# Three moves in the issue order of a two-layer attention and expert kernel: the first context's load, the experts' ranks, the last attention output

## The chip, the cores and the metric

The kernel runs on one core of a Trainium2 chip. The core has five engines that work side by side and wait for each other by semaphores: PE (TensorE, matrix products and transposes into PSUM), DVE (VectorE), ACT (ScalarE), POOL (GpSimd) and SP (SyncE, which here only issues transfers). PEld in a profile is PE's loading of weights, which overlaps its matmuls. The metric is device time in microseconds for one execution, as the median of the runs.

## The reference

The inputs are 32 sequences of 64 rows of 512 numbers (2048 rows in all), and a context of the same shape. Two layers follow each other, each a cross-attention and a feed-forward part, each added to the rows:

```
x = x + attention0(layernorm(x), context)     # 32 heads of 128, 8 key/value groups
x = x + ffn0(layernorm(x))                    # up 1024, relu squared, down, a latent branch, layernorm
x = x + attention1(rmsnorm(layernorm(x)), context)   # 32 heads of 16, 8 key/value groups
x = x + experts(layernorm(x))                 # 8 experts, each row takes its best two
```

The expert part, which most of the change touches, is

```python
logits = x @ W_gate + b_gate
_, top_idx = jax.lax.top_k(logits, TOP_K)        # TOP_K = 2
y_all = jax.nn.relu(jnp.einsum('bsd,edh->bseh', x, W_e) + b_e)
y = jnp.take_along_axis(y_all, top_idx[..., None], axis=2)
return y.mean(axis=2)
```

## The kernel before

The 2048 rows are four chunks of 512 (`c`), each chunk four tiles of 128 rows (`xs[i]`), which stay in SBUF from the first load to the end. All numbers are float32.

**Start.** SP issues the loads in their written order (L187 to 193): the four x tiles of chunk 0, the first group's weights by `load_attn0` (keys `wk`, queries `wq`, values `wv`, output `wo`), then the context of chunk 0 (`load_ctx`, 1 MB, the transposed context in four blocks of 128 by 512), then chunk 1's rows and context, then the rest. PE begins with the transposes of chunk 0's normalized rows (`attn0_in`, pt_a), goes on to keys (`attn0_keys`, pk_a) and values (`attn0_values`, pv_a), which multiply the context, then to seven quarters of a query product in Strassen's form (`attn0_queries`, pqx_a, pqy_a, pqz_a, pqv_a), whose sums of weight quarters POOL makes (`left_sums` for `wq`, `right_sums` for `wo`). DVE closes the query quarters into qT_a (L500), copies the values (L478), and makes the row statistics of later chunks (`row_stats`).

**The second attention and the routing.** A loop over 33 batches (`i`, from L1317 on; `c, b = divmod(i, 8)`) is a pipeline written out by hand. In iteration i come, in this order: the masked keys for batch i+2 (POOL), the scores of batch i (PE sixteen small matmuls sc_b; DVE maximum and subtraction, mx_b and at_b; ACT the exponential), the transposes of batch i-1 (pt_v), one half of a query product for the next chunk (`attn1_queries`, pq_b), the routing step of chunk c-1 that a table names for this b, the row work of chunk c+2, the mixing of batch i-1 (`attn1_mix`: PE po, ACT a copy, logarithm and exponential, POOL four instructions L994 to L998), the output product of an earlier pair of batches (`attn1_out`: PE pp, DVE the addition into x, L1012), and up to two scatters from a list of waiting ones (`route_row`). In the last chunk (c = 3) there are no queries left, and `attn1_out` comes every second iteration as a whole.

The routing of a chunk has these steps (`route_step`): normalize rows (`rows0`, `rows2`), transpose them (`turn0`, `turn2`), multiply by the gate (`logits`, gp_e), then `ranks` and `places`. `ranks` is `route_keep`: four transposes (lg_e) and eight dependent DVE instructions from the logits to keep_e, which marks the two best experts of each row. `places` is `route_places`: two small matmuls (cnt_e) that count the rows ahead of each row in its expert's list, the running sums on DVE, and at_e, the row numbers for the scatters. Each scatter (`route_row`, xg<-...,at_e) is an indirect transfer that POOL issues. Chunks 0 to 2 form the first group of lists, chunk 3 the second.

**The expert blocks.** After the loop `load_rows` reads the sorted rows back (xr<-xg, on SP, after all scatters of the group), `block_turn` transposes a block of 128 rows (px, ACT copies it to xT), and `block_expert` multiplies it by its expert's weights (py). At m = 0 the output product of the last tile (`attn1_out(NC * TT - 1, ...)`) is issued behind the first block's transposes. 46 blocks follow each other; their results are gathered and added.

**What sets the order.** A scheduler orders each engine's instructions at compile time by its own estimate of times, lower positions in the program first. `pin` (and `accumulate_next`) keeps an instruction behind the one written before it on its engine. The matmuls, the routing on DVE, and the mixing on POOL are pinned; the statistics, the additions of L1012, and the loads on SP are not. PSUM tiles are handed out in turn: "tr" (transposes, logits, counts) has two buffers, "mm" (products) two in this part.

## Time and profile before

| what | us |
|---|---|
| median of 3 runs | 2020.13 (2019.36 to 2022.64) |
| the profiled execution | 2020.86 |
| its span, first to last instruction | 2019.2 |
| PE busy | 1939.5 (96%) |
| DVE busy | 1011.8 (50%) |
| ACT busy | 494.5 (24%) |
| POOL busy | 474.4 (23%) |
| DMA from HBM / to HBM | 94.44 MB / 58.20 MB |

Starts in a timeline are counted from the first instruction. A group's line gives its start, its length, engine, line of the code, operation and tiles, how many instructions were merged, and in brackets how long the engine had been idle and which instruction ended that. The chain of work that ended last is 91% PE and 5% DVE. The page in 40 slices shows where the engines have gaps (each digit is a tenth of a slice of 50.5 us):

```
PE   6999999999999999999999999999999999869995
DVE  8445445445456445345345355365546676652324
POOL 5010010010032110110111120144136545541024
```

The first attention runs to about 1241 us (its last output product), the first feed-forward part to about 1513, the batches of the second attention from 1560 to about 1808, the expert blocks to 1996, and the last gathers and additions to 2019.

### The profile page before, as it was taken

Reading aid. Unit: us, or ns where it says so; the run is one execution under the profiler, and the core shown is the slowest. Engines: PE = TensorE matmul, PEld = TensorE weight load, DVE = VectorE, ACT = ScalarE, POOL = GpSimd, SP = SyncE. Lnnn points to the kernel's source line nnn. Section 1 sums busy time; section 2 is a strip of 40 time slices with the busy share of each in tenths; the row PEclk is TensorE's granted clock in tenths of the full one; section 3 lists DMA queues with packets and bytes.
Section 4 is the critical chain, followed back from the end, with each engine's and each line's share of the span. In section 5 each row is a group of like instructions: output and inputs, shape, how many; then the busy total and the mean of one; then the engine's idle time right before and its main releaser. Section 6 shows DMA issues by size and latency. Waiting matters only on the chain.

```text
span 2019.2 us, 26458 instructions
## 1 busy us (share of the span) xinstructions
PE 1939.5 (96%) x10576; PEld 1537.1 (76%) x10576; DVE 1011.8 (50%) x1961; ACT 494.5 (24%) x935; POOL 474.4 (23%) x502
## 2 busy tenths in 40 slices
PE   6999999999999999999999999999999999869995
PEld 5888888888888888888888887778787767545442
DVE  8445445445456445345345355365546676652324
ACT  1211211211212211111111112221113656433221
POOL 5010010010032110110111120144136545541024
PEclk9999999999999999999999999999999999889998
DMA  9993110110120110110110013000014002225457
GB/s 319 284 294 106 35 53 18 35 53 20 54 74 8 45 37 17 52 39 15 52 42 13 21 58 105 1 11 1 1 46 163 17 22 69 84 84 177 155 165 233
DMA packets 138233, 155.39 MB, mean 77 GB/s; under 512 B 5120, under 2 KB 88896, under 8 KB 138112
## 3 DMA queue, kind: packets, MB, share of 16 engines
q1 hardware_dynamic: 126096, 124.53, 19.8%
q0 software_dynamic: 5392, 17.11, 2.6%
q10 hardware_dynamic: 6624, 12.06, 1.6%
q8 instruction: 85, 1.39, 0.3%
q14 instruction: 36, 0.29, 0.0%
HBM read 94.44 MB, written 58.20 MB: 76 GB/s over the span
## 4 chain that ended last, share of the span: by engine, by line
PE 91%; DVE 5%; ACT 1%; DMA 1%; POOL 1%; issue 1%; POOLq 0%; SPq 0%; DVEq 0%; ACTq 0%
PE ppx_o L424 11%; PE pqx_a L424 8%; PE py L105 8%; PE sc_a L105 6%; PE pv_a L105 5%; PE ppz_o L424 5%; PE pqz_a L424 5%; PE pk_a L105 5%; PE po_o L105 3%; PE pp L105 3%; PE pdx_f L424 3%; PE ppy_o L424 3%; PE pqy_a L424 3%; PE pqv_a L424 3%; PE phx_f L424 2%; PE pq_b L105 2%
## 5 line engine op out<-in xcount | busy, mean ns | idle before, releaser
L105 PE MATMUL py<-arena,xT 128*128 x368 | 165.7, 593 | 0.0
L406 POOL TENSOR_TENSOR arena<-weights 128x512 f32<-128x512 f32 x16 | 20.7, 1295 | 563.2 <-PE ppz_o L424 563.2
L365 ACT ACTIVATE at_a<-at_a 128x512 f32<-128x512 f32 x64 | 40.4, 631 | 444.0 <-DVE at_a L364 444.0
L105 PEld LDWEIGHTS pv_a<-weights,arena 128*128 128x128 f32 x1024 | 119.4, 192 | 15.3 <-issue 15.3
L424 PE MATMUL ppx_o<-weights,oT_o 128*128 128x256 f32 x512 | 122.8, 383 | 0.1
L424 PE MATMUL pqz_a<-arena 128*128 128x256 f32 x512 | 121.0, 379 | 1.8 <-DVE qT_a L500 1.8
L105 PE MATMUL pk_a<-arena,weights 128*128 128x512 f32 x256 | 117.7, 603 | 3.6 <-issue 3.6
L424 PE MATMUL pqx_a<-arena,weights 128*128 128x256 f32 x512 | 121.0, 379 | 0.0
L105 PEld LDWEIGHTS sc_a<-kT_a,qT_a 128*128 128x128 f32 x1024 | 119.4, 192 | 1.7
L493 ACT ACTIVATE u_a<-pqx_a,bq 128x256 f32<-128x256 f32 x192 | 80.5, 470 | 163.2 <-PE pqx_a L424 163.2
L105 PE MATMUL pv_a<-weights,arena 128*128 128x128 f32 x1024 | 119.5, 275 | 0.0
L105 PE MATMUL sc_a<-kT_a,qT_a 128*128 128x64 f32 x1024 | 117.9, 273 | 0.0
L105 PEld LDWEIGHTS py<-arena,xT 128*128 128x128 f32 x368 | 66.3, 190 | 65.5 <-issue 65.5
L478 DVE COPY v_a<-pv_a 128x512 f32<-128x512 f32 x32 | 22.1, 690 | 179.8 <-PE pv_a L105 179.8
L584 DVE TENSOR_TENSOR x<-ppx_o,x 128x512 f32<-128x512 f32 x128 | 86.8, 678 | 45.7 <-PE ppx_o L424 43.9
L424 PEld LDWEIGHTS pqz_a<-arena 128*128 128x128 f32 x512 | 97.2, 190 | 15.3 <-issue 2.2
L424 PEld LDWEIGHTS ppx_o<-weights,oT_o 128*128 128x128 f32 x512 | 94.8, 190 | 12.0 <-ACT oT_o L574 0.5
L424 PEld LDWEIGHTS pqx_a<-arena,weights 128*128 128x128 f32 x512 | 94.8, 190 | 11.6
L500 DVE TENSOR_TENSOR qT_a<-pqz_a,u_a 128x512 f32<-128x512 f32 x64 | 44.2, 691 | 112.3 <-ACT u_a L493 80.3
L1217 DVE TENSOR_TENSOR y<-py,weights 128x512 f32<-128x512 f32 x46 | 31.8, 691 | 119.7 <-PE py L105 119.3
L105 PEld LDWEIGHTS pk_a<-arena,weights 128*128 128x128 f32 x256 | 49.3, 194 | 52.9 <-issue 51.5
L396 POOL TENSOR_TENSOR arena<-weights 128x512 f32<-128x512 f32 x18 | 23.2, 1290 | 243.5 <-PE pqz_a L424 240.5
(337 smaller groups left out, 3823.2 us busy)
## 6 DMA issues: line engine op xcount, KB each, us to landing
xg<-zero SPq DMA_DIRECT2D x8, 3072.0 KB, 18.0
weights<-in_Wq SPq DMA_DIRECT2D x16, 1024.0 KB, 5.3
weights<-in_Wo SPq DMA_DIRECT2D x16, 1024.0 KB, 5.2
xr<-xg SPq DMA_DIRECT2D x46, 256.0 KB, 3.4
yg<-y ACTq DMA_DIRECT2D x46, 256.0 KB, 3.0
weights<-in_Wkv SPq DMA_DIRECT2D x32, 256.0 KB, 2.8
arena<-in_ctxT SPq DMA_DIRECT2D x8, 1024.0 KB, 5.1
xg<-zero SPq DMA_DIRECT2D x8, 1024.0 KB, 13.0
```

What stands on the lines that cost most here:

```text
L105: nc.tensor.matmul(ps, lhsT, rhs, start=(i == 0), stop=(i == len(pairs) - 1))
L365: nc.scalar.activation(dst, dst, AF.Exp, scale=scale)
L396: engine.tensor_tensor(s1, a21, a22, ALU.add)
L406: engine.tensor_tensor(t1, b12, b11, ALU.subtract)
L424: nc.tensor.matmul(ps[:, m, :], left[:, k, m * P : (m + 1) * P], right[:, k, :], start=first and m == i == k == 0, stop=i == len(pairs) - ...
L478: nc.vector.tensor_copy(v, pv)
L493: nc.scalar.activation(u[:, m * 256 : (m + 1) * 256], ps[:, m * 256 : (m + 1) * 256], AF.Identity, bias=bq[:, 4 * g + 2 * heads + m : 4 * ...
L500: nc.vector.tensor_tensor(q5[:, heads, :, 4 * half : 4 * half + 4, :], ps.rearrange("p (m b q) -> p m b q", m=2, q=64), u.rearrange("p (m ...
L584: nc.vector.tensor_tensor(dst, ps.rearrange("p (m n) -> p m n", m=2), dst, ALU.add)
L1217: pin(nc.vector.tensor_tensor(y, py, be1[:, bass.ds(v[1], 1), :], ALU.add))
```

## The change

Three edits, with no change to what is computed.

1. `load_attn0` gets a hook behind the key weights, and loads `wv` ahead of `wq` in every visit. For the first visit the hook loads chunk 0's context. The order at the start was x0 to x3, wk, wq, wv, wo, ctx0, x4...; it becomes x0 to x3, wk, ctx0, wv, wq, wo, x4....
2. `ranks` leaves the two routing tables. It is issued one batch earlier, at the end of the iteration with b = 5 (b = 3 for the last chunk of queries), behind `attn1_out`, while `places` stays in the iteration with b = 6 (b = 4). Three chunks pass through this; chunk 3's routing runs between the expert blocks and is as before.
3. At m = 0 `attn1_out` of the last tile is issued ahead of `block_turn`, no longer behind it.

```diff
-    def load_attn0(g, slot):
+    def load_attn0(g, slot, between=lambda: None):
         ...
         nc.sync.dma_start(wk, rows(a["Wkv"][:, g * P : (g + 1) * P]))
+        between()
+        nc.sync.dma_start(wv, rows(a["Wkv"][:, (NG + g) * P : (NG + g + 1) * P]))
         nc.sync.dma_start(wq, rows(a["Wq"][:, g * 512 : (g + 1) * 512]))
-        nc.sync.dma_start(wv, rows(a["Wkv"][:, (NG + g) * P : (NG + g + 1) * P]))
         nc.sync.dma_start(wo, rows(a["Wo"][g * 512 : (g + 1) * 512, :]))
         ...
         if c == 0:
-            w_next = load_attn0(0, 0)
-        if c < 2:
+            w_next = load_attn0(0, 0, between=lambda: load_ctx(0, ctx_q[0]))
+        if c == 1:
             load_ctx(c, ctx_q[c])
...
     ROUTE = {
-        0: ["rows0"], 1: ["turn0"], 3: ["rows2"], 4: ["turn2"], 5: ["logits"], 6: ["ranks", "places"]
+        0: ["rows0"], 1: ["turn0"], 3: ["rows2"], 4: ["turn2"], 5: ["logits"], 6: ["places"]
     }
-    ROUTE_LAST = {0: ["rows0"], 1: ["turn0"], 2: ["turn2"], 3: ["logits"], 4: ["ranks", "places"]}
+    ROUTE_LAST = {0: ["rows0"], 1: ["turn0"], 2: ["turn2"], 3: ["logits"], 4: ["places"]}
...
                 attn1_out(k, oTs[k], (1 - i % 2,))
+        if 0 < c < NC and b == (5 if c + 1 < NC else 3):
+            route_step(c - 1, "ranks")
         if c == NC - 1 and b == 1:
             route_step(c - 1, "rows2")
...
-            turned = block_turn(i, j, xr[i])
             if m == 0:
                 attn1_out(NC * TT - 1, oTs.pop(NC * TT - 1), (0, 1))
+            turned = block_turn(i, j, xr[i])
```

## The prediction

> **What bounds the kernel now.** I read the page first: TensorE (PE) is busy for 96% of the span, and the rows by slice show full PE and full clock from about 50 to 1650 us. Nothing of this change lies there.

> ```profile
> PE 1939.5 (96%) x10576; PEld 1537.1 (76%) x10576; DVE 1011.8 (50%) x1961; ACT 494.5 (24%) x935; POOL 474.4 (23%) x502
> PEclk9999999999999999999999999999999999889998
> ```

> So time can only come out of PE's few waits. The view of waits, kept to PE, lists them (line, releaser: total us, times, longest):

> ```profile
> PE cnt_e L105 <- DVE keep_e L1058: 10.9, 3, 4.5
> PE px L1196 <- DMA xr<-xg: 5.3, 1, 5.3
> PE pp L105 <- POOL mix_last L998: 4.0, 2, 3.3
> PE pk_a L105 <- issue: 3.6, 1, 3.6
> PE pqz_a L424 <- DVE qT_a L500: 1.8, 1, 1.8
> ```

> cnt_e is the first matmul of `route_places`; keep_e ends `route_keep` (the ranks). The three waits fall at 1654.2 (3.18 us), 1717.6 (3.15) and 1766.9 (4.54). The timelines of PE and then of DVE round the second (start, us, engine line op, tiles):

> ```profile
> 1715.29 1.89 PE L105 MATMUL pq_b<-rT_b,weights 128*128 128x256 f32 x8
> 1717.02 0.60 PE L314 MATMUL lg_e<-ident,gp_e 128*128 128x128 f32 x4
> 1720.77 0.60 PE L105 MATMUL cnt_e<-keep_e,before 128*128 128x32 f32 x2 [3.15 <-DVE keep_e L1058]
> ```
> ```profile
> 1717.66 0.29 DVE L317 TENSOR_REDUCE lgs_e<-lg_e 128x32 f32<-128x128 f32 x1 [0.38 <-PE lg_e L314]
> 1720.44 0.18 DVE L1058 TENSOR_SCALAR keep_e<-rank_e 128x32 f32<-128x32 f32 x1
> 1724.04 0.17 DVE L1115 CAST at_e<-two_e 128x8 int32<-128x8 f32 x1
> ```

> PE turns the logits, then stands while DVE runs eight dependent instructions (1717.66 to 1720.62, 2.96 us). Each wait also costs clock. The view by stretches (the stretch and its length, busy us and count of PE, weight loads, DVE, ACT and POOL, granted clock, DMA share, GB/s):

> ```profile
> 1720.50:1727.30 6.80, 6.53 (x28) 4.05 (x28) 2.18 (x14) 1.42 (x3) 2.79 (x5) 0.50 0.10 39
> 1749.30:1752.00 2.70, 0.01 (x2) 0.04 (x1) 2.35 (x14) 0.69 (x2) 0.80 (x1) 0.86 0.94 344
> 1752.00:1758.00 6.00, 6.00 (x45) 4.18 (x46) 3.77 (x7) 3.54 (x7) 0.51 (x1) 0.50 0.65 220
> 1797.00:1799.00 2.00, 0.20 (x2) 0.09 (x1) 1.94 (x4) 1.15 (x3) 0.00 (x0) 1.00 0.22 84
> ```

> After the second wait PE works for 6.8 us at half clock; after the first and third it is about 3.4 us.

> **Edit 1, the first context.** The first context chunk, ninth in the order, is issued at 5.46 and lands 13.5 us later (18.96); pk_a starts at 19.04, though the transposes ahead of it end at 15.41. In the new order it has the bytes ahead of it that wq has now (four x tiles, wk), and wq lands at 3.17 + 9.5 = 12.67. wv keeps its bytes: 3.72 + 9.8 = 13.5. wq takes wo's place (4.27 + 12.0 = 16.27), wo the context's (18.96). So pk_a starts at about 15.45, **3.6 us earlier**. What is late next: POOL's first wq sum ran at 16.55 (0.28 to spare), its first wo sum at 18.22 (now 0.74 of waiting, with three wq sums behind it on POOL); the last of those ended at 24.49 and its reader, the last query quarter, comes not before 35, so this costs nothing. Later visits also load wv ahead of wq; tens of us of PE work hide that.

> [...] pk_a's weight loads come 0.855 us apart up to 23.44; in the steady state eight matmuls take 3.44 us, 0.43 each. [...] If the opening moves along, keys and values end 3.6 us earlier (28.6 to 25.0). If it stays at 24.1, the eight pk_a take 6.84 (to 22.3), eight of 32 pv_a run at half pace, and the end is 26.8: 1.85 gained. The trace has one start only, so I take the middle, **2.7**. It must pass DVE, too: qT_a (L500) at 40.12 releases pqz_a, and DVE is busy with other chunks' statistics, placed ahead of it as fill, from 22 to 41. If that order stays, nothing is gained; if the planner pulls the closes forward with the matmuls, the 1.8 of pqz_a may go as well. Bounds: -0.7 (POOL's wait passed on) to 5.4.

> **Edit 2, ranks one batch ahead.** It moves four transposes and eight DVE instructions, no DMA, from behind the next batch's scores (0.67), turn (1.0) and queries (1.73) to ahead of them. SP and POOL have nothing in it, but POOL's scatters wait for its end. The chain stands on DVE ahead of the next softmax (four instructions, 2.77 us), and that ahead of the places (2.37). DVE's sum is the same, so scatters can start only 1 to 1.5 us earlier: what PE loses least, DVE decides.
> - Chunk 1's batch 5/6: lg ends at 1650.7, keep at 1653.9, while PE has scores, turn and queries to 1654.1: no wait. Softmax ends at 1656.7; only then DVE reads cnt_e (1657.0), and the second pt_b transpose needs that PSUM buffer: a new wait of 1.9. Then po, and pp behind the query copy, which ACT does after the second exp: 1660.3 for the next scores against 1663.41, 3.1 gained. POOL starts its run of five scatters and a mix (9.65 us) at 1659.5 instead of 1660.6, so the next mix starts 0.85 after it could. It is ahead of the scatter for which h_e waits. I take **2.6**; bounds 1.1 (scatters' advance) and 4.6 (wait and its clock).
> - Chunk 2's: keep at 1717.35, PE there at 1717.55. Softmax to 1720.15, exp 1720.85, query copy 1721.25; pp waits 2.3 for it. Scores at 1723.2 against 1727.31: **4.1**, bounds 1.5 and 6.5.
> - Chunk 3's: no queries stand between. Keep at 1767.9 to 1768.6, PE there at 1766.3: a wait of 1.8 to 2.5 remains of 4.5. DVE's places end at 1773.1 to 1773.8 (now 1774.55). The next pp waits for POOL's mix_last, which now stands behind three scatters (1774.83 to 1781.2). ACT's part of that mix would be ready at 1772.9, ahead of the scatters. Mix first: pp at 1775.7, 5.6 gained; one scatter first, as in chunk 2: 4.1; three: 1.3. I take **3.5**, one scatter and a late keep.

> [...] The trace is harsher: the 2.7 us up to 1752.0 were enough for 6.8 us at half, while two waits of 1.8 and 0.7 near 1798 kept 1.00. 1.9 and 2.3 are nearer the row that kept it, so the sum has no loss; if it falls at each, it is 1.7 to 3.4 us a time, inside the bounds.

> **Edit 3, last output ahead of the first block.** PE timeline:

> ```profile
> 1808.88 1.09 PE L1196 MATMUL px<-ident,xr 128*128 128x128 f32 x4 [5.31 <-DMA xr<-xg]
> 1809.76 5.06 PE L105 MATMUL pp<-weights,mix_last 128*128 128x256 f32 x16
> ```

> POOL's last mix ends at 1807.81, so sixteen pp and two DVE adds can start 1.0 us sooner and fill the wait for xr. The row loads on SP stay ahead. What is lost: the first block's ACT copy (0.58) lay beside pp and is now half covered by the second px (0.44), 0.3 shows. **0.7**, bounds -0.3 and 1.3.

> **Sum.** 2.7 + 2.6 + 4.1 + 3.5 + 0.7 = 13.6. Behind the last edit PE runs blocks without a wait to 1996, so all of it reaches the end. The profiled execution took 2020.86 (span 2019.2 and 1.66 round it): 2007.3; it stood 0.7 over the median of the runs, 2020.13, which gives **2006.6**.

> **Rivals.**
> - *DVE sets these stages.* For it: the scatters advance by just 1.1, 1.5 and 1.3, and DVE has no gap between 22 and 41. Against it: PE, not POOL, is late for most of chunk 2. Gain 0 + 1.1 + 1.5 + 1.3 + 0.7 = 4.6: 2015.5. Chance 0.17, half of which and a little more is over the threshold.
> - *All waits go with their clock*, and the planner reorders luckily: 5.4 + 4.6 + 6.5 + 5.6 + 1.3 = 23.4, 1996.7. The PSUM buffer behind pt_b speaks against it. Chance 0.13.
> - *Slower: the ranks ahead of the softmax.* Waits of 1.9, 2.3 and 2.5 (6.7) each bring 3.4 of lost clock (10.2), and the softmax, late by 2.96 at three places, holds the score buffers of the batch after as well (8.9): 25.8 against what goes, 10.9 and half of 13.7 us at half clock, 17.7. With nothing from edit 1 and 0.7 from edit 3 that is 7.4 more: 2027.5. It decides once the new waits pass about 2.7 us each. DVE's idle 3.2 us per batch round 1727 speaks against it. Chance 0.06.
> - *Not done as written*: the loads on SP are not pinned; but they were issued in their written order, so I give this no share of its own.

> The forecast has 0.64. About 0.2% (4 us) is what a measurement here tells from no change. Faster 0.64 + 0.13 + 0.10 = 0.87, same 0.07, slower 0.06. Eight in ten: from 2000, part of the way to the best case, to 2016, which takes in the first rival.

> **What would show it.** pk_a near 15.5 and PE at its next scores (now 42.9) about 2.7 earlier; keep_e gone from PE's waits twice, about 2 us left once; new waits at pt_b and pp of the same batches; mix_last ahead of most scatters in the last chunk; pp before px. Wrong if pqz_a waits 4 us or more (edit 1 empty), or if granted clock is 0.5 behind the small new waits.

## The result and the profile after

| kernel | median us | runs | ratio to before, 95% interval |
|---|---|---|---|
| before, run beside it | 2019.74 | 4 (2017.86 to 2022.64) | |
| after | 2008.01 | 4 (2006.76 to 2011.58) | 0.9944 [0.9926, 0.9961] |

The change makes the kernel 11.7 us faster by the medians; 2006.6 was predicted, with 2000 to 2016 as the range. The profiled execution of after took 2011.58 and has a span of 2009.9 (9.3 below the 2019.2 of before); it was the longest of its four.

The page of after, the rows that answer to the two shown of before:

```profile
PE 1939.5 (96%) x10576; PEld 1539.5 (77%) x10576; DVE 1014.9 (50%) x1961; ACT 494.4 (25%) x935; POOL 475.0 (24%) x502
PEclk8999999999999999999999999999999999989998
```

PE's busy time is the same to a tenth of a us, so what went is PE's waiting, about 9 us net; a low clock counts as busy time (12.34 of 13.70 us at 0.50 in the second stretch below). In the clock's row the first digit fell from 9 to 8, and of the two neighbouring 8s (slices from 1716 to 1817 us in before) the first is a 9 now: something was lost at the very start, something won in the last chunks. The waits of PE in after (line, releaser: total us, times, longest):

```profile
PE pp L105 <- POOL mix_last L999: 5.3, 3, 4.3
PE pp L105 <- ACT qT_b L1023: 4.4, 5, 1.6
PE pqz_a L425 <- DVE qT_a L501: 4.4, 1, 4.4
PE cnt_e L105 <- DVE keep_e L1059: 3.6, 3, 2.0
...
PE pt_e L918 <- DVE h_e L909: 2.7, 1, 2.7
...
PE pt_b L918 <- ACT rT_b L920: 1.9, 2, 1.6
```

Three rows of before are gone or small: keep_e held PE for 10.9 us and now for 3.6, the 5.3 for xr and the 3.6 at pk_a have left the list. But others grew: the second pqz_a from 1.8 to 4.4, mix_last from 4.0 to 5.3, the query copy (qT_b) from 3.0 to 4.4, and pt_b from 0.3 to 1.9. The view by stretches says at which clock PE worked behind them (stretch, its length, busy us and count of PE, weight loads, DVE, ACT, POOL, granted clock, DMA share, GB/s):

```profile
14.70:18.30 3.60, 3.60 (x11) 1.69 (x10) 2.65 (x2) 0.59 (x1) 3.02 (x4) 1.00 1.05 385
35.40:49.10 13.70, 12.34 (x50) 11.66 (x51) 9.54 (x22) 0.98 (x2) 5.39 (x4) 0.50 1.07 324
1660.20:1663.60 3.40, 3.40 (x21) 1.97 (x14) 2.02 (x10) 1.89 (x4) 1.63 (x3) 0.50 0.05 18
1727.00:1730.50 3.50, 1.90 (x19) 1.30 (x11) 3.19 (x14) 2.42 (x6) 3.12 (x5) 1.00 0.41 155
1796.70:1803.60 6.90, 5.58 (x13) 4.51 (x14) 0.42 (x1) 0.00 (x0) 1.18 (x3) 0.51 0.90 260
```

The first keys (14.7 on) run at full clock. From 35.4 PE works for almost 14 us at half clock: this is the price of the 4.4 us wait at pqz_a. The waits near 1727 cost no clock, those before 1660 and at 1797 did.

Where the 9.3 us of the profiled pair came from, by how far each start lies ahead of the same start in before:

| place | ahead by, us | so this part gave |
|---|---|---|
| chunk 1's first pk_a (48.18, now 49.78) | -1.6 | edit 1: -1.6 |
| last twelve scores of the third batch behind chunk 1's places (1678.43, now 1679.00) | -0.6 | edit 2, chunk 1: 1.0 |
| scores two batches behind chunk 2's places (1734.45, now 1730.99) | 3.5 | edit 2, chunk 2: 4.0 |
| first half of the last pp but one (1795.12, now 1785.27) | 9.9 | edit 2, chunk 3: 5.9, and 0.5 of clock at pt_e |
| first py (1815.09, now 1805.56) | 9.5 | edit 3: -0.3 |

So edit 2 carries it, edit 1 even cost time in this execution, and edit 3 gave nothing. (The expectations below have 1.1 for chunk 1, counted from a start just ahead of its ranks.)

### The profile page after: what moved, and what is told of

Same layout as the page of the kernel before. It is cut to its first block, busy times and chain, and to the rows that moved or that the text cites. A ratio compares the mean times of both kernels' runs of the same rounds, so it can differ in the third digit from the quotient of the medians.

```text
span 2009.9 us, 26460 instructions
## 1 busy us (share of the span) xinstructions
PE 1939.5 (96%) x10576; PEld 1539.5 (77%) x10576; DVE 1014.9 (50%) x1961; ACT 494.4 (25%) x935; POOL 475.0 (24%) x502
## 4 chain that ended last, share of the span: by engine, by line
PE 90%; DVE 6%; ACT 2%; POOL 1%; issue 1%; DMA 1%; POOLq 0%; SPq 0%; DVEq 0%; ACTq 0%
PE ppx_o L425 11%; PE pqx_a L425 8%; PE py L105 8%; PE sc_a L105 6%; PE pqz_a L425 6%; PE pv_a L105 6%; PE ppz_o L425 5%; PE pk_a L105 5%; PE po_o L105 3%; PE ppy_o L425 3%; PE pdx_f L425 3%; PE pqv_a L425 3%; PE pqy_a L425 3%; PE pp L105 3%; PE phx_f L425 2%; PE pq_b L105 1%
## 5 line engine op out<-in xcount | busy, mean ns | idle before, releaser
L105 PE MATMUL py<-arena,xT 128*128 x368 | 165.8, 593 | 0.2 <-ACT xT L1200 0.2
L105 PEld LDWEIGHTS pv_a<-weights,arena 128*128 128x128 f32 x1024 | 119.4, 192 | 15.3 <-issue 15.3
L105 PEld LDWEIGHTS sc_a<-kT_a,qT_a 128*128 128x128 f32 x1024 | 122.7, 196 | 1.8
L105 PE MATMUL sc_a<-kT_a,qT_a 128*128 128x64 f32 x1024 | 121.0, 278 | 0.0
L105 PE MATMUL pv_a<-weights,arena 128*128 128x128 f32 x1024 | 119.5, 275 | 0.0
L105 PEld LDWEIGHTS py<-arena,xT 128*128 128x128 f32 x368 | 66.2, 190 | 66.0 <-issue 65.5
L105 PE MATMUL pk_a<-arena,weights 128*128 128x512 f32 x256 | 115.2, 593 | 0.0
L105 PEld LDWEIGHTS pk_a<-arena,weights 128*128 128x128 f32 x256 | 48.5, 191 | 47.4 <-issue 45.9
```

Of the source, the lines that this page charges most:

```text
L105: nc.tensor.matmul(ps, lhsT, rhs, start=(i == 0), stop=(i == len(pairs) - 1))
```

## The experiments

**The three edits one by one.** Each kernel has the lines of one edit of the change and no other; `all_three` has them all and is the kernel after once more, beside the parts.

```diff
+        between()
+        nc.sync.dma_start(wv, rows(a["Wkv"][:, (NG + g) * P : (NG + g + 1) * P]))
         nc.sync.dma_start(wq, rows(a["Wq"][:, g * 512 : (g + 1) * 512]))
```

> Edit 1 alone (context ahead of wv, wq, wo). Theory A, clock phase: the close of qT_a for the second pqz_a comes about 4.2 us earlier in every execution, but how long PE waits for it, and whether the clock falls behind that wait, depends on when the clock opens in that execution. Where it opens late (pk_a at half pace) PE waits about 1 us and 4.2 us are gained; where it opens early (pk_a at full pace) PE waits over 3.4 us, the clock falls to half for up to 13.7 us and 1 to 2 us are lost. So single times should spread over some 5 us, and the median lie 0 to 4 us below before. Rival B, a constant gain: 2.7 to 3.6 us below before in each execution, spread no wider than that of before.

```diff
-    6: ["ranks", "places"]
+    6: ["places"]
...
+        if 0 < c < NC and b == (5 if c + 1 < NC else 3):
+            route_step(c - 1, "ranks")
```

> Edit 2 alone (ranks one batch ahead). Theory A: from the trace of the changed kernel, chunk 1 about 1.1, chunk 2 about 4.0, chunk 3 about 5.9 us (11 in all, with 0.4 of clock between), so 10 to 12 us below before, nearly the whole gain. Rival B: DVE's unchanged sum of work sets these stages, 4 us or less below before, and the rest of the measured gain came from edit 1.

```diff
-            turned = block_turn(i, j, xr[i])
             if m == 0:
                 attn1_out(NC * TT - 1, oTs.pop(NC * TT - 1), (0, 1))
+            turned = block_turn(i, j, xr[i])
```

> Edit 3 alone (last attention output ahead of the first block). Theory A: the pp matmuls start about 1 us sooner after the last mix, but run deeper in the half-clock window that the wait before them brings, so that the first py comes 0 to 0.7 us sooner; the time can't be told from before (within 1.5 us). Rival B: what PE did at half clock was the loss, and filling the wait shortens it: 2 us or more below before.

> The changed kernel itself once more, beside its three parts. Both theories: 2006 to 2012 us, 0.992 to 0.996 of before. Theory A (clock phase): its profile, if the clock opens at another time than in the first one (14.96 us), shows the second pqz_a after another wait, and PE's next keys (pk_a of chunk 1, 49.78 in the first profile, 48.18 before) between 44 and 50; the sum of the three parts alone equals the whole within 2 us.

| kernel | median us | runs | ratio to before |
|---|---|---|---|
| before | 2021.0 | 35 | |
| e1_context_only | 2020.05 | 22 | 0.9994 [0.9987, 1.0] |
| e2_ranks_only | 2011.27 | 6 | 0.9948 [0.9931, 0.9964] |
| e3_output_only | 2021.75 | 14 | 0.9998 [0.9988, 1.0009] |
| all_three | 2009.41 | 6 | 0.994 [0.9923, 0.9957] |

By the ratios the parts are 1.2, 10.5 and 0.4 us, 12.1 together, and the whole is 12.1: they add. Edit 1 and edit 3 alone can't be told from nothing.

What edit 1 gives differs by execution. In the six profiles that have it and leave DVE's order as it was, PE waited 3.6 to 4.4 us at the second pqz_a. In four of them chunk 1's pk_a started between 46.25 and 46.74, in two (after and warm_last_output, below) at 49.78 and 50.44. What differs is the clock behind the wait: 0.50 from 35.4 to 49.1 in after, 0.55 from 36 to 43 in e1_context_only (pk_a at 46.59), 0.83 from 36.0 to 46.3 in all_three (46.25). Without edit 1 it started between 48.15 and 48.18 in three profiles. Theory A of e1_context_only had also expected waits of about 1 us where the clock opens late; none was seen, and the times of that kernel spread by 6.4 us, those of before by 9.8.

**What hides edit 1.** PE in after, at the start (start, us, engine line op, tiles):

```profile
14.75 3.71 PE L105 MATMUL pk_a<-arena,weights 128*128 128x512 f32 x8
...
30.50 1.89 PE L425 MATMUL pqv_a<-arena,weights 128*128 128x256 f32 x8
36.76 3.75 PE L425 MATMUL pqz_a<-arena 128*128 128x256 f32 x8 [4.37 <-DVE qT_a L501]
...
49.78 3.60 PE L105 MATMUL pk_a<-arena,weights 128*128 128x512 f32 x8
```

The context came in time: pk_a starts right behind the transposes, and its eight matmuls take 3.71. PE stood before the second pqz_a at 32.4. That matmul adds onto the tile that the close of the first pqz_a reads on DVE, and DVE in after has this:

```profile
33.51 0.66 DVE L346 BATCH_NORM_STATS2 st_a<-x 128x6 f32<-128x512 f32 x1
...
35.93 0.68 DVE L501 TENSOR_TENSOR qT_a<-pqz_a,u_a 128x512 f32<-128x512 f32 x1
```

DVE isn't idle ahead of the close: it works through statistics without a gap. Six of them between 30.3 and 35.1 belong to chunks 2 and 3, whose attention comes only after the eight visits of chunks 0 and 1; the scheduler had put them there as fill. The next two kernels hold these behind the last close of the first queries, on DVE alone; the orders on PE, POOL and SP stay as in the whole change. `stats_without_edit1` is the same with edits 2 and 3 alone.

```diff
     def attn0_in(c):
-        mv, rstd = chunk_stats(c, f"a{c}")
+        with tc.issue_after(closes[3].ins) if c > 1 else ExitStack():
+            mv, rstd = chunk_stats(c, f"a{c}")
...
         def close(heads, half, ps, u):
-            nc.vector.tensor_tensor(...)
+            closes.append(nc.vector.tensor_tensor(...))
```

> The whole change, and on DVE the statistics of chunks 2 and 3 are held behind the last close of the first queries. If their place ahead of the closes is what took edit 1's gain: the second pqz_a follows pqv_a at about 32.3 without a wait and at full clock (the waits were 4.4 and 3.8 us in the two profiles of the whole change), pk_a of chunk 1 starts at about 40 instead of 46.3 to 49.8, and the run takes 6 us less than the whole change (6 below all_three's 0.994 of before, so about 0.991). Rival: something else is late next there (POOL's sums of Wq, or h_a of chunk 1): a wait of over 2 us stays, and at most 2 us come off.

> The same, but without edit 1 (context behind the weights again). If DVE's order alone hid edit 1, then with DVE free edit 1 is worth its full 3.6 us of earlier context: this run is 3.6 to 4.5 us slower than stats_behind_closes, and its second pqz_a has lost the wait of 1.0 to 2.3 us. Rival: edit 1 is empty by itself, and all of the gain is in the order on DVE: the two differ by less than 2 us.

| kernel | median us | runs | ratio to before (2021.21 beside these) |
|---|---|---|---|
| stats_behind_closes | 2002.42 | 4 | 0.9907 [0.9892, 0.9922] |
| stats_without_edit1 | 2010.25 | 5 | 0.9945 [0.9931, 0.9958] |

PE and one close on DVE in stats_behind_closes:

```profile
33.65 1.97 PE L425 MATMUL pqz_a<-arena 128*128 128x256 f32 x8
...
41.29 3.60 PE L105 MATMUL pk_a<-arena,weights 128*128 128x512 f32 x8
```
```profile
32.81 0.69 DVE L505 TENSOR_TENSOR qT_a<-pqz_a,u_a 128x512 f32<-128x512 f32 x1 [0.93 <-ACT u_a L497]
```

The close now waits for ACT and no longer for DVE's queue, pqz_a follows without a wait, PE keeps its full clock (1.00 from 31.7 to 49.0), and chunk 1's pk_a starts at 41.29. Without edit 1 it starts at 47.15 in the same order. So the two things need each other: freeing DVE without the early context gives next to nothing (2010.25 against the 2011.27 of the ranks alone), the early context without DVE about 1.2, both together 7.8 (2010.25 - 2002.42). This is more than the 3.6 of the landing, and more than the 3.6 to 4.5 expected. In stats_without_edit1 PE stood 4.9 us before pk_a and then ran its eight matmuls in 6.05, against 4.25 in stats_behind_closes. The four transposes ahead of the wait took 0.71 there and 1.11 in stats_behind_closes; by this pace the clock was already open, and fell in the wait:

```profile
19.91 6.05 PE L105 MATMUL pk_a<-arena,weights 128*128 128x512 f32 x8 [4.89 <-issue]
```

By chunk 1's pk_a the two profiles are 5.9 apart (47.15 and 41.29). The 2 us between 5.9 and 7.8 are within the intervals.

**Chunk 1's places: the order on PE.** The new pt_b wait of 1.57 is for the buffer that cnt_e holds until DVE reads it. This kernel puts the transposes ahead of the count.

```diff
+        if 0 < c < NC and (c, b) != (1, 6):
             for step in ...: route_step(c - 1, step)
...
                 turn_step(c + 2, 0)
+                if c == 1: route_step(0, "places")
                 rows_step(c + 2, 2)
```

> The whole change, and in batch 6 of chunk 1 the two transposes pt_b of chunk 3 stand ahead of cnt_e on PE. If the buffer that cnt_e holds and the late keep_e cause the waits there (0.97 for keep_e and 1.57 at pt_b): both go, 2.5 us of waiting and up to 1.7 of half clock, less a wait for the query copy that may show at pp: 1.5 to 3.5 us less than the whole change. Rival: DVE's softmax sets the next scores anyway, and the wait moves to pp or to pt_v: within 0.7 us.

2012.38 us (5 runs), ratio 0.995 [0.9935, 0.9965]: nothing gained, the rival is right so far. Both waits became one of 2.72 at cnt_e, for ACT's copy of pt_b, which stands on ACT behind the exponential of the late softmax. The next scores came as long behind those of batch 6 as in after (12.17 us against 12.23), and in both pp came out slow behind the wait (2.74 and 2.92 us, against 1.99 a batch earlier), and two batches on the scores stood 2.31 us for at_b, up to 1677.79. The next study meets the same wait and takes it up.

**POOL beside the rank chain, and the scatters behind it.** In chunk 1 of after, DVE needed 4.2 us from the logits to the end of keep_e; in before it was 2.96. One instruction of it, in all_three and then in mix_behind_ranks, where POOL's mix of that batch waits for keep_e:

```profile
1650.12 0.93 DVE L1049 TENSOR_TENSOR cmp_e<-lgs_e 128x256 f32<-128x256 f32 x1 [0.48 <-POOL mix L997]
```
```profile
1644.91 0.42 DVE L1062 TENSOR_TENSOR cmp_e<-lgs_e 128x256 f32<-128x256 f32 x1 [0.48 <-DVE lgs_e L1051]
```

```diff
-        pin(nc.gpsimd.tensor_tensor(t, t, y, ALU.mult))
...
+        def close(behind=None):
+            first = pin(nc.gpsimd.tensor_tensor(t, t, y, ALU.mult))
+            if behind is not None:
+                tc.add_manual_dep(first.ins, behind.ins.name, waits, reason="DVE's ranks first")
...
             route_step(c - 1, "ranks")
+            if later:
+                later(ranked[0])
```

Only batch 4's mix of chunk 1 is held so; it is written behind the ranks of that iteration (`later` is its `close`), and `behind` is the instruction that makes keep_e. The kernel stands on `stats_and_warm` (below).

> stats_and_warm, and in batch 5 of chunk 1 POOL's mix starts only after DVE's keep_e. If POOL's mix at the same time is what stretched the rank chain of chunk 1 (4.2 us from the logits to the end of keep_e, instead of 3.0 elsewhere): the chain takes 3.0, cnt_e's wait of 0.97 is gone, and the scores of the next batch start 1.2 us earlier, up to 2.9 where the clock holds as well. The mix ends 2 us later, and its reader comes 14 us later. Rival: DVE's chain is long for another reason, or the exp and the query copy on ACT set the next scores anyway: chain still about 4 us, or the time within 0.7 us of stats_and_warm.

The two lines show the same comparison, 0.93 us beside POOL and 0.42 without it; the 0.48 of idling ahead of it stayed, so that was not POOL's doing, whatever releaser is named. The chain took 3.35 (1643.91 to 1647.26), cnt_e's wait went, PE kept its clock (the pp behind pt_b took 1.99, 2.34 in stats_and_warm), and the next scores started at 1653.56 instead of 1655.99. Yet the time is 2001.16 (5 runs), 0.9896 [0.988, 0.9913], against 2001.27 for stats_and_warm: the rival's result, though the chain did shorten. PE and DVE of mix_behind_ranks show where it went:

```profile
1670.84 0.71 PE L105 MATMUL sc_b<-bo,qT_b 32*128 32x128 f32 x12 [2.46 <-DVE at_b L958]
```
```profile
1669.64 0.55 DVE L914 TENSOR_SCALAR arena<-x,mv_e,rs_e 128x512 f32<-128x512 f32 x1 [4.06 <-DMA xg<-arena,at_e]
```

DVE stands before a write of h_e: the rows of chunk 1's tokens go into the buffer from which the scatters of chunk 0's tokens still read. The softmax, at_b, is queued behind it, and PE's scores wait for at_b. These scores (of batch 1 of chunk 2; the next expectation calls them batch 0's) lay 17.2 to 18.8 us behind the first scatter in this profile and in every other but that of the next kernel. It gives chunk 1's rows a buffer of their own; for that one expert is loaded with the last three, not with the first five.

```diff
-prep["h"] = route_rows if c < NC - 2 else t8(f"h_{n}")
+prep["h"] = (route_rows, arena[:, 4])[c] if c < NC - 2 else t8(f"h_{n}")
...
-    load_experts(range(5))
+    load_experts(range(4))
...
-            load_experts(range(5, NE))
+            load_experts(range(4, NE))
```

> mix_behind_ranks, and the normalised rows of chunk 1's tokens (h_e, written on DVE from batch 0 of chunk 2 on) get a buffer of their own, in place of the one that the scatters of chunk 0's rows still read; the expert that lay there (the fifth) is loaded with the last three. If that buffer is what gives back the gain of edit 2 in chunk 1 (the scores of batch 0 of chunk 2 stood 17.2 to 18.8 us behind the first scatter in every kernel, and in mix_behind_ranks they wait 2.5 us for at_b, which stands behind h_e on DVE): DVE's two waits for the scatters (1.9 and 4.1 us there) go, PE's wait of 2.5 goes, and the run takes 2.5 to 4 us less than mix_behind_ranks, about 1997.5 to 1999, ratio 0.988. Rival: POOL's run of scatters and mixes sets the pace there whatever the buffer (pp waits for POOL's mix instead), or the next clock window takes it back: within 1 us.

```profile
1667.82 0.73 PE L105 MATMUL sc_b<-bo,qT_b 32*128 32x128 f32 x16
```

The scores wait no more and end 3.0 us earlier (1668.55, not 1671.55), and the run takes 1997.93 (5 runs, 1997.56 to 1999.06), 0.9884 [0.9868, 0.99]. By the medians this is 3.2 less than mix_behind_ranks, by the ratios 2.4, with intervals that overlap; two of the five runs of mix_behind_ranks were as fast (1996.98 and 1997.98). That the buffer made the wait is shown by the trace; how much of the time it is worth stays open between these figures.

**How the parts of edit 2 share.** The ranks go ahead in the last chunk alone:

```diff
-    6: ["places"]
+    6: ["ranks", "places"]
...
-        if 0 < c < NC and b == (5 if c + 1 < NC else 3):
+        if c == NC - 1 and b == 3:
             route_step(c - 1, "ranks")
```

> The whole change, but the ranks go ahead only in the last chunk (for chunk 2's tokens); in chunks 1 and 2 they stand where they were. By the starts in the two traces the three places gave 1.1, 4.0 and 5.9 us: so this is 5.1 us slower than the whole change, 0.9965 of before. By the prediction's terms (2.6, 4.1, 3.5) it is 6.7 slower, 0.9973. A rival, that the last chunk's waits take up what the first two places give (POOL's queue fixes the end of the stage): about as fast as the whole change, 0.994.

2014.1 us (10 runs), 0.9968 [0.9957, 0.9979]. With edits 1 and 3 and the last chunk alone there is a little over half of the gain, as the starts said (0.9965). The interval still holds 0.9973, so it doesn't exclude the prediction's shares; it does exclude that the last chunk makes all of it (0.994).

**The clock behind a wait, and edit 3.** PE of all_three at the last output, then of warm_last_output, where 28 transposes, whose result nobody reads, stand ahead of it on PE:

```profile
1795.97 6.53 PE L105 MATMUL pp<-weights,mix_last 128*128 128x256 f32 x16 [4.31 <-POOL mix_last L999]
```
```profile
1796.56 3.28 PE L1392 MATMUL idle<-ident 128*128 128x128 f32 x28
1800.94 3.72 PE L105 MATMUL pp<-weights,mix_last 128*128 128x256 f32 x16 [1.11 <-POOL mix_last L999]
```

```diff
             if m == 0:
+                idle = ps_tr("idle")
+                for k in range(28):
+                    pin(nc.tensor.transpose(idle[:, (k % 4) * P : (k % 4 + 1) * P], ident, ident))
                 attn1_out(NC * TT - 1, oTs.pop(NC * TT - 1), (0, 1))
```

> The whole change, and 28 transposes of the identity into a PSUM tile that nobody reads stand on PE ahead of the last attention output, so that PE works while it waits for mix_last (4.3 us there). If the clock that falls behind this wait is what took edit 3's gain: the 16 pp take about 3.5 us instead of 6.4 at granted clock 1.00, and the run takes 2.5 to 3 us less than the whole change. Rival: the clock falls by its own time and not by the wait, or the first block waits for its rows anyway: within 0.7 us, or slower by what the transposes delay.

> Both of the last call's gains in one kernel: the whole change, the statistics of chunks 2 and 3 behind the first closes, and the 28 transposes ahead of the last output. They lie 1750 us apart and PE is full between them, so they should add: 6.8 and 2.4 us less than the whole change, about 2000.0, ratio 0.989. Rival: the clock's windows fall elsewhere behind the shift, and up to 3 us of half clock come back in other places: 2003.

warm_last_output took 2006.62 (5 runs), 0.9928 [0.9914, 0.9942]; the sixteen pp took 3.72 instead of 6.53 at granted clock 1.00, and the first py came 13.8 us behind the second half of the previous tile's pp (1791.97), not 16.6 (1787.01 in all_three). The ratio is 2.4 us better than that of the whole change, with intervals that overlap; what is shown is the 2.8 between these two traces. With the statistics moved as well (stats_and_warm, 2001.27, 4 runs, 0.9907 [0.989, 0.9924]) only 1.2 by the medians was added to stats_behind_closes, not 2.4, and by the ratios nothing. The profiles give a reason: in stats_behind_closes the same pp took 5.11, where all_three took 6.53, so there was 1.4 to be had (5.11 less 3.72), not 2.8.

## Why the prediction was right, and where not

The total was right to 1.4 us, and in good part by luck. The main idea held: the ranks' waits were the time to be had (keep_e fell from 10.9 us to 3.6). But of the five terms, 2.7, 2.6, 4.1, 3.5 and 0.7, the profiled pair showed -1.6, 1.0, 4.0, 5.9 and -0.3, and 0.5 of clock besides; only chunk 2's was right, and a term too small made up for some of those too large.

- **Edit 1, 2.7 predicted; 1.2 measured alone, -1.6 in the profiled pair.** The landing was right (pk_a at 14.75; 15.45 was predicted), and the clock's opening did move along (14.96, from 24.08 in before): pk_a's eight matmuls took 3.71, not 6.17, and those behind them were full-paced, so PE reached the second pqz_a at 32.4, 6.8 sooner than in before (40.95 less its wait of 1.80). The step that failed is taking "the middle" of two cases for the clock, which no run shows (the eight pk_a took 3.62 to 4.25 in after, e1_context_only, all_three and stats_behind_closes): the question was not the clock but the condition written behind it, that it "must pass DVE". The scheduler did pull the close forward, past two of the eight statistics of chunks 2 and 3 and most of the arithmetic behind them, but six stayed ahead of it: DVE released pqz_a at 36.76, 4.2 sooner and no more, and pqz_a waited 4.37, past the 4 us that were named as the sign of an empty edit 1. It should have been the likely case: the trace of before showed DVE without a gap from 22 to 41. What the prediction missed altogether is the loss: such a wait also closes the clock (0.50 from 35.4 to 49.1 in after). In after pqz_a, sc_a and pt_a took 3.75, 6.93 and 2.93 us, in before 1.97, 3.84 and 1.92; these 5.9 turn 4.2 gained into the 1.6 lost. stats_behind_closes shows the cause.
- **Edit 2, chunk 1: 2.6 predicted, 1.0 measured in the profiled pair.** That is close to the lower bound, "1.1 (scatters' advance)", but by luck. The scatters advanced by 0.4 us only: the first one came 17.1 us behind the scores of batch 5 in after, 17.5 in before. The reason is the chain of ranks, which the prediction took over at 2.96 us from another place; moved, it ran beside POOL's mix and took 4.2. The rest of the 1.0 is spread: in all_three the stretch from the scores of batch 5 to those late scores took 35.8 us, of which 3.46 for the slow pp, and in before 35.4, with 2.93 for it (1.99 at full clock). What the prediction had wrong is the path: the wait that ends last here is for a buffer. The scatters read the rows buffer, DVE waits for them before it writes the next rows (h_e) there, and the softmax stands behind that write on DVE. In after:

```profile
1677.80 0.55 DVE L909 TENSOR_SCALAR arena<-x,mv_e,rs_e 128x512 f32<-128x512 f32 x1 [3.20 <-DMA xg<-arena,at_e]
```

  So only what the scatters advance is paid out; own_rows_for_chunk1 took that hold away.
- **Edit 2, chunk 2: 4.1 predicted, 4.0 measured.** The waits came where they were expected, 0.69 for keep_e and 0.62 and 1.60 for the query copy, without loss of clock (1.00 at 1727).
- **Edit 2, chunk 3: 3.5 predicted, 5.9 measured.** The wait for keep_e that remained was 1.97 (1.8 to 2.5 predicted). The term that was too small is POOL's: one scatter was placed ahead of mix_last, and one did stand there, but the other three instructions of the mix were done before it (1768.44 to 1770.24), mix_last ended at 1772.16, and the pp behind the places did not wait for POOL at all, as these lines of after and before show. By its gain it was the case named "mix first: 5.6".

```profile
1764.38 0.38 PE L105 MATMUL cnt_e<-keep_e,before 128*128 128x32 f32 x2 [1.97 <-DVE keep_e L1059]
...
1772.65 3.79 PE L105 MATMUL pp<-weights,mix_last 128*128 128x256 f32 x16
```
```profile
1771.39 0.38 PE L105 MATMUL cnt_e<-keep_e,before 128*128 128x32 f32 x2 [4.54 <-DVE keep_e L1058]
...
1781.25 5.41 PE L105 MATMUL pp<-weights,mix_last 128*128 128x256 f32 x16 [3.27 <-POOL mix_last L998]
```

- **Edit 3, 0.7 predicted, nothing measured (0.9998).** pp does go first and the wait for xr is gone. But in before the wait for xr was 5.3 us long and swallowed 3.0 of the 6.8 us of half clock (from 1805.84; px at 1808.88); in after the wait is 4.3 and swallows 1.3 of 6.8 (from 1796.72; pp at 1798.02). PE begins a us sooner and works slowly for as much longer. The sum had no term for the clock here, and warm_last_output shows it.
- **The small waits.** They were priced without loss of clock, and half clock behind them was named as a sign of being wrong. In chunk 1 it came: the two waits there (0.97 and 1.57, close together) brought 3.4 us of half clock in after (0.50 at 1660.2), and the waits of all_three and e2_ranks_only are the same to 0.01; from the second pt_b to the next scores PE took 5.15 us in after, 6.29 in all_three and 3.51 in e2_ranks_only, where pt_b, po and pp all ran at full pace. Those of chunk 2 brought none in after (1.00 at 1727). So such a pair cost 0, 1.6 or 2.8 us, by the run, and the sum should have had a term for it.
- **The rivals.** The first (DVE sets these stages, and the gain is what the scatters advance) was right for chunk 1 alone. The second (all waits go) failed where the prediction said, at pt_b, which waited 1.57. The slower one needed waits of more than 2.7 us each behind the ranks; the longest was 1.97.

## What to carry to other kernels

A transfer that lands sooner, or work that is ordered sooner, pays only as far as the next engine's queue lets it through (edit 1 gave 1.2 us, and 7.8 together with a freed DVE): follow the gain to the next engine that was busy without a gap, and look whether what fills that engine could wait. Price a wait of PE with the clock that it may close (13.7 us of half clock behind the 4.37 at pqz_a in after), and price a step that is moved with what then runs beside it (the ranks of chunk 1: 4.2 us beside POOL's mix, 3.35 without it). When several waits are removed in a row, look for the one buffer whose release is tied to something slow (here the scatters, for which DVE stood 3.20 us in after), for it sets how much of the others is paid out.
